# The seam between layer 0's mixing and layer 1's hop: the last tile's norm, transposes and projection reordered

## The chip, the cores and the metric

The kernel runs on one core of one Trainium2 chip. The metric is the device time of one execution in microseconds (us); it is compared by the median of several runs. The core's engines work side by side, each through its own queue in order: TensorE (PE, with its weight loads shown as PEld), VectorE (DVE), ScalarE (ACT), GpSimd (POOL) and SyncE (SP), which here only issues DMAs.

## The reference

Two layers over a graph of 2048 nodes, with 8 batches of 64 features. The adjacency is sparse (self loops, row-normalised).

```python
# layer 0: three Chebyshev terms, weights per node mixed from 16 embeddings
w = einsum('nd,dkio->nkio', embedding, weight); b = einsum('nd,do->no', embedding, bias)
As = [I, A, 2 A A - I]
x_g = einsum('knm,bmc->bnkc', As, x)
x = layernorm(x + einsum('bnki,nkio->bno', x_g, w) + b)
# layer 1: x, A x, 2 A A x - x, and again the last two, concatenated, times one weight
x = layernorm(x + concat(x, A x, 2 A A x - x, A x, 2 A A x - x) @ weight + bias)
```

So the adjacency is applied four times, one after the other: twice in layer 0 (hops 1 and 2), twice in layer 1 (hops 3 and 4). Between hops 2 and 3 stands the mixing of layer 0: for each node, 64 features of three terms times 16 weight matrices, weighted by the node's embedding and summed.

## The kernel before, in words

The function `pattern` holds the whole path that is measured. Nodes are cut into 16 tiles of 128 (NT = 16); tile t lies on the 128 partitions, with 8 x 64 features along the free dimension.

**Hops.** Hops 2 and 3 are built by `seven_products` (L586): seven products of half-size matrices in place of eight, each product in 8 steps (kk = 0 to 7). A step has parts with leads: `sum_y` (lead 5), `y_high` and `load_sum` (lead 4), `y_low` (3), `operands` (2) and `use` (0). `run` (L265) goes over the steps; at step i it issues part p of step i + lead, so a step's operands are made some steps ahead of its matmuls. `load_sum` (L636) has SP load a matrix block into a buffer of the pool `rawp` (5 buffers); `operands` (L647) casts it on ScalarE (L652) into a buffer of `spool` (4 buffers); `y_high` (L625) and `y_low` (L633) split the moving features into a high part on ScalarE (L234) and a low part on VectorE (L238); `use` (L657) issues 8 matmuls (L664). Hop 3's first product has its accumulators in `sums3[0]`; `sums3[1]` lies idle in that product, and `transpose` and `project` borrow it.

**Layer 0's mixing.** The loop at L861 goes over the tiles. `mix0` (L402) issues eight pieces of matmuls (L409) for a tile. A piece (g, i) covers batch group g. With i below 2 it is `by_batch`: its 8 weight matrices are read out of PSUM by ScalarE (L423, 8 instructions), times the embedding, into two `aside` tiles of `rawp`; GpSimd adds those up (`sum_aside`, L440, three instructions, after both such pieces of the group) and then into the sum (`add_aside`, L445). With i of 4 or 5 it is `by_four`: VectorE adds four matrices from PSUM straight into the sum (L433, 4 instructions). The list `at[n]` holds what is issued ahead of piece n: it is the order by hand of the other engines' queues. PSUM has four pairs of banks (`bank`, L84), shared by pieces, transposes, projections and hop accumulators. Tile t's operands (`operands`, L725) take a `rawp` buffer and two `spool` buffers until its last matmul.

`mix0` returns `layernorm` (L359), a generator. Its first step, right after the tile, sums (L362, L363, VectorE) and centres (L365, GpSimd). Its three further steps, called n1, n2, n3 in the loop, are issued in the next tile: n1 squares (L353, ScalarE), n2 sums them (L370, VectorE) and takes the root (L372, ScalarE), n3 takes the reciprocal (L374, VectorE) and ends on GpSimd (L375 to L380), where L380 writes the normalised tile. Then `transpose` (L303) does eight transposes on TensorE (L300), which ScalarE reads out into `hT` (L306), and `project` (L458) does 16 matmuls with layer 1's weights (L466) and six copies on ScalarE (L475).

For tiles 1 to 14 the previous tile's transposes are issued ahead of piece 7 and its projection after piece 7. The last tile, 15, is different: it issues n1, n2, n3 of tile 14 ahead of pieces 1, 2 and 3, and between them makes operands for hop 3 early (`early`, L846, moves named parts of a step forward: for steps 0 and 1 all parts but the matmuls, for steps 2, 3 and 4 the high and low parts). Tile 14's transposes are issued after step 1 of hop 3 (`last_transposed`, L791) and its projection after step 2 (`last_projected`, L794); tile 15's after steps 5 and 6. Tile 15's own n1, n2, n3 are put into `todo` (L900), from which `run` takes two entries after each step.

What sets the order: ScalarE, VectorE and GpSimd instructions marked `ordered`, and SP's loads, keep the order in which the program issues them. A pool's buffer is handed to the next tile that asks, when the work that last used it is done.

Of the kernel before, what the change touches and what calls it, by code (L numbers as in the profile page):

```python
# [20 lines left out]
NT = N // P  # L21
# [18 lines left out]
def pattern(  # L40
# [24 lines left out]
    def pool(stack, name, bufs, **kw):  # L65
        return stack.enter_context(tc.tile_pool(name=name, bufs=bufs, **kw))
# [17 lines left out]
    def bank(name):  # L84

        return psum.tile([P, 2, 512], F32, tag="ps", name=name)
# [9 lines left out]
    def bc(s, t):  # L96
        return z[s][t].rearrange("p (b c) -> p b c", c=C)
# [29 lines left out]
    def ordered(ins):  # L127
        if in_order:
            tc.keep_in_program_order(ins)
# [161 lines left out]
    def by_half(tt):  # L291
        return tt.rearrange("p j (h n) -> p h j n", h=2)

    def transposed(src, pt=None):

        pt = bank("pt") if pt is None else pt
        for j in range(B // 2):
            for h in range(2):
                q = slice(h * C, (h + 1) * C)
                nc.tensor.transpose(pt[:, h, j * C : (j + 1) * C], src[q, 2 * j * C : 2 * (j + 1) * C], ident[q, q])  # L300
        return pt[:, :, : B // 2 * C].rearrange("p h (j n) -> p h j n", n=C)

    def transpose(src, tag, pt=None):  # L303

        tt = xcpool.tile([P, B // 2, P], F32, tag="ln_xc", name=tag)
        ordered(nc.scalar.copy(by_half(tt), transposed(src, pt)))  # L306
        return tt
# [81 lines left out]
    def begin_sum(t):  # L389

        acc = work.tile([P, B, C], F32, tag="acc", name="acc")
        for g in range(2):
            ordered(nc.gpsimd.tensor_tensor(
                acc[:, 4 * g : 4 * g + 4, :].rearrange("p (j i) c -> p j i c", j=2),
                bc(0, t)[:, 4 * g : 4 * g + 4, :].rearrange("p (i j) c -> p j i c", j=2),
                ebias[:, t : t + 1, :].unsqueeze(1).to_broadcast([P, 2, 2, C]), ALU.add,
            ))
        return acc
# [59 lines left out]
    def project(t, hT, pus=None):  # L458


        for g in range(2):
            pm = bank("pu") if pus is None else pus[g]
            for i in range(2):
                for j in range(2):
                    q = slice(j * C, (j + 1) * C)
                    nc.tensor.matmul(  # L466
                        pm[:, j, i * 3 * C : (i + 1) * 3 * C], lhsT=hT[q, 2 * g + i, :], rhs=v[q],
                        start=True, stop=True,
                    )
            got = pm[:, :, : 6 * C].rearrange("p j (i k c) -> p j i k c", i=2, k=3)  # L470

            order = ["p (i j) c -> p j i c", "p (j i) c -> p j i c", "p (j i) c -> p j i c"]
            to = [bc(k, t)[:, 4 * g : 4 * g + 4, :].rearrange(order[k], j=2) for k in range(3)]
            for k in range(3):
                ordered(nc.scalar.copy(to[k], got[:, :, :, 2 - k, :]))  # L475

    def add_bias(t):
        to = bc(2, t)
        ordered(nc.vector.tensor_tensor(to, to, bias1.unsqueeze(1).to_broadcast([P, B, C]), ALU.add))
# [232 lines left out]
    def times_r(t):  # L712
        to = z2[:, t, :].rearrange("p (j n) -> p j n", n=P)
        r = rrow[:, t * P : (t + 1) * P].unsqueeze(1).to_broadcast([P, B // 2, P])
        ordered(nc.gpsimd.tensor_tensor(to, to, r, ALU.mult))  # L715
# [9 lines left out]
    def operands(t, quick=False):  # L725

        xt = work2.tile([P, B // 2, P], F32, tag="t0", name="xt")
        load(nc.sync, xt, xT[t])
        tt = [None] * 3

        def begin(k, src):
            where, tag = ((rawp, "raw"), (spool, "s"))[k != 2]
            high = hpool.tile([P, B // 2, P], F32R, tag="hl", name="hl")
            pair = where.tile([P, 2, B // 2, P], F32R, tag=tag, name="parts")
            tt[k] = [high, pair[:, 0], pair[:, 1]]
            return parts(src, tt[k], by_half if k == 1 else lambda to: to, quick)

        def of_x():
            yield from begin(0, xt)

        def of_hop(pt=None):
            yield from begin(1, transposed(z[1][t], pt))

        def of_second():
            yield from begin(2, by_pair(z[2][t]))

        return tt, of_x(), of_hop, of_second()
# [40 lines left out]
    last_h = {}  # L788
    sums3 = []

    def last_transposed(t):  # L791
        last_h["T"] = transpose(last_h[t], "hT", sums3[1][0])

    def last_projected(t):  # L794
        project(t, last_h["T"], (sums3[1][1], sums3[1][0]))
        if t < NT - 1:
            return
        layer0.close()
        t_pool = pool(tpool, "fzT", 1, reuse_waits="tile")
        for a in range(2):  # L800
            for c in range(2):
                zT[a, c] = t_pool.tile([P, 4, B * C], F32, tag=f"zT{a}{c}", name="zT")
# [22 lines left out]
    def quarter_back(a, b, which):  # L825
# [7 lines left out]
        return work_here + [lambda n=n: two(n) for n in range(0, 8, 2)]  # L833

    third = seven_products(0, to_zT, sums3, {
        (0, 1): [lambda: last_transposed(NT - 2)],
        (0, 2): [lambda: last_projected(NT - 2)],
        (0, 5): [lambda: last_transposed(NT - 1)],
        (0, 6): [lambda: last_projected(NT - 1)],
        **{(2 + t // KK, t % KK): [lambda t=t: add_bias(t)] for t in range(NT)},  # L840
        3: quarter_back(1, 1, 1), 4: quarter_back(0, 1, 0), 5: quarter_back(0, 0, 1),
    }, wait=2)
# [3 lines left out]
    def early(i, *kinds):  # L846

        got = third_got.setdefault(i, {})
        for lead, part in sorted(third[i], key=lambda part: -part[0]):
            if part.__name__ in kinds:  # L850
                part(got)
        third[i] = [part for part in third[i] if part[1].__name__ not in kinds]

    def go(it):
        return lambda: next(it)

    y, s = ("y_high", "y_low"), ("load_sum", "operands")
    acc, h, norm = first_tile[5], None, None
    tt = first_tile[0]
    coming = operands(1)  # L860
    for t in range(NT):  # L861
        got, last = {}, t == NT - 1
        at = [[] for _ in range(9)]
        n1, n2, n3 = [lambda: next(norm)] * 3 if t else [nothing] * 3

        if not last:
            following, of_x, of_hop, of_second = coming
            of_hop = of_hop()
            at[1] += [go(of_x)] * (1 if t else 3)
            at[2] += [go(of_hop), n1, go(of_hop), go(of_hop), n2]  # L870
            if t + 2 < NT:
                at[2] += [lambda: times_r(t + 2)]
                at[4] += [lambda: got.update(coming=operands(t + 2))]
            at[3] += [n3, go(of_second), lambda: got.update(acc=begin_sum(t + 1))]
            at[4] += [go(of_second), go(of_second)]
            at[6] += [(("sum", "add"), 0)]
            at[7] += [lambda: got.update(hT=transpose(h, "hT"))] if t else []
            pieces = [(0, 0), (0, 4), (0, 5), (1, 2), (0, 1), (1, 3), (1, 4), (1, 5)]
        else:
            at[1] += [n1, lambda: early(0, *y, *s)]  # L880
            at[2] += [n2, lambda: early(1, *y, *s)]
            at[3] += [n3, (("sum",), 0), lambda: early(2, *y)]
            at[4] += [lambda: early(3, *y)]
            at[5] += [lambda: early(4, *y)]
            at[6] += [(("add",), 0)]
            at[7] += [(("sum",), 1)]
            at[8] += [(("add",), 1)]
            pieces = [(0, 0), (0, 1), (0, 4), (1, 0), (0, 5), (1, 1), (1, 4), (1, 5)]
        norm_now = mix0(t, tt, acc, at, pieces)
        if 0 < t < NT - 1:  # L890
            project(t - 1, got["hT"])
        if "coming" in got:
            coming = got["coming"]
            next(coming[1])
            next(coming[1])
        norm = norm_now
        last_h[t] = h = next(norm)
        if not last:
            tt, acc = following, got["acc"]
    todo.extend([nothing] * 4 + [lambda: next(norm)] * 3)  # L900
# [425 lines left out]
def gnn_kernel(tc, x, xT, adj, diag, rcols, bias, pack, w0, out):  # L1326
    nc = tc.nc
    with tc.tile_pool(name="flag", bufs=1) as fpool:
        flag = fpool.tile([1, 1], I32, tag="flag", name="flag")
        odd = pattern(tc, x, xT, adj, diag, rcols, bias, pack, w0, out, flag)  # L1330
        with tc.If(odd > 0):
            general(tc, x, adj, bias, pack, w0, out)
# [47 lines left out]
```

## Time and profile before

| | |
|---|---|
| median of 3 runs | 765.45 us (764.99 to 766.03) |
| profiled execution, its own time | 765.98 us |
| its span, first to last instruction | 764.2 us, granted TensorE clock 0.998 |
| TensorE matmuls busy | 754.5 us (99%), 6634 instructions |
| VectorE, ScalarE, GpSimd busy | 559.0, 407.4, 269.6 us |
| tile 15 on TensorE | 509.08 to 526.1 us |
| hop 3 from its first matmul | 526.18 us |

A line of a timeline reads: start, duration, engine, line, operation, output <- inputs, partitions x elements, count; in brackets the idle time ahead and what ended it. A line of several instructions gives their common stretch. "SPq" is a DMA being issued from SP. Matmuls overlap, so the spacing of their starts, not their duration, is what one costs. The buffers' numbers are left out of names: `aside`, `raw`, `parts` and `hl` each stand for several.

### The profile page before, as it was taken

The page shows a single profiled execution, that of the slowest core. Times are in us where ns is not written, and L with a number is a line of the kernel's source. Part 1 is how long each engine was busy: PE and PEld are TensorE (multiplying, and loading weights), DVE is VectorE, ACT ScalarE, POOL GpSimd, SP SyncE. Part 2 cuts the span into 40 slices and gives each one's busy share as a digit, 9 for nine tenths or more (in the row PEclk, how much of TensorE's full clock was granted, in tenths as well). Part 3 has the DMA queues.
Part 4 walks back from the last instruction along what each step waited for, and adds up shares of the span by engine and source line. Part 5 has one row for each costly group of instructions (what it writes and reads, how often), then busy time and mean ns, then how long its engine had stood idle before and what let it go on. Part 6 is the DMA issues. An engine that isn't in the chain of part 4 may idle for free.

```text
span 764.2 us, 16926 instructions
## 1 busy us (share of the span) xinstructions
PE 754.5 (99%) x6634; PEld 658.8 (86%) x6634; DVE 559.0 (73%) x1159; ACT 407.4 (53%) x896; POOL 269.6 (35%) x297
## 2 busy tenths in 40 slices
PE   9999999999999999999999999999999999999996
PEld 6888888888889999999999999998788888888885
DVE  5768867678757888888888888875688648668663
ACT  4456533877855555555555555556887663112111
POOL 0000000000026877777788787766100000011441
PEclk9999999999999999999999999999999999999999
DMA  9998996555510000000000000002454444566631
GB/s 316 364 394 274 351 313 223 162 169 163 170 66 22 24 17 15 17 16 15 16 17 16 15 16 3 2 30 78 129 166 149 132 154 143 175 174 177 205 125 45
DMA packets 73558, 96.69 MB, mean 127 GB/s; under 512 B 4864, under 2 KB 48384, under 8 KB 73344
## 3 DMA queue, kind: packets, MB, share of 16 engines
q1 hardware_dynamic: 62064, 76.66, 31.7%
q10 hardware_dynamic: 11408, 18.89, 6.7%
q8 instruction: 54, 0.88, 0.5%
q14 instruction: 32, 0.26, 0.1%
HBM read 76.65 MB, written 18.87 MB: 125 GB/s over the span
## 4 chain that ended last, share of the span: by engine, by line
PE 95%; POOL 2%; ACT 1%; DVE 1%; DMA 0%; issue 0%; POOLq 0%; DVEq 0%
PE pm L409 34%; PE accT L664 25%; PE acc L254 15%; PE a L254 10%; PE accT L254 6%; PE pu L466 2%; PE pt L300 1%; POOL aside L440 1%; PE first L143 1%; PE accT L816 1%; ACT aside L423 1%; DMA raw<-corner 0%; POOL xc L380 0%; ACT s L652 0%; DVE acc L433 0%; ACT z L475 0%
## 5 line engine op out<-in xcount | busy, mean ns | idle before, releaser
L433 DVE SCALAR_TENSOR_TENSOR acc<-pm,pack_sb,acc 128x256 f32<-128x256 f32 x376 | 181.1, 482 | 40.1 <-PE pm L409 28.1
L664 PE MATMUL accT<-s,hl 128*128 128x512 f32 x896 | 206.6, 391 | 0.8 <-ACT s L652 0.8
L409 PE MATMUL pm<-wh,hl 64*128 64x512 f32 (+1 forms) x1332 | 204.1, 303 | 0.0
L409 PE MATMUL pm<-wm,parts 64*128 64x512 f32 (+1 forms) x1332 | 199.7, 296 | 0.0
L409 PE MATMUL pm<-wl,parts 64*128 64x512 f32 (+1 forms) x1332 | 199.6, 296 | 0.0
L664 PEld LDWEIGHTS accT<-s,hl 128*128 128x128 f32 x896 | 167.3, 188 | 36.7 <-ACT s L652 1.2
L652 ACT CAST s<-raw 128x1024 fp32r<-128x1024 bf16 x104 | 110.0, 1058 | 43.4 <-ACT hl L234 23.4
L409 PEld LDWEIGHTS pm<-wh,hl 64*128 64x128 f32 x1332 | 126.8, 187 | 4.6 <-issue 0.4
L409 PEld LDWEIGHTS pm<-wl,parts 64*128 64x128 f32 x1332 | 126.7, 187 | 4.3
L409 PEld LDWEIGHTS pm<-wm,parts 64*128 64x128 f32 x1332 | 126.4, 187 | 4.4
L254 PE MATMUL acc<-hl,s 128*128 128x512 f32 x512 | 116.9, 390 | 0.0
L254 PEld LDWEIGHTS acc<-hl,s 128*128 128x128 f32 x512 | 96.3, 188 | 20.5 <-ACT hl L234 0.3
L423 ACT ACTIVATE aside<-pm,pack_sb 128x128 f32<-128x128 f32 x272 | 74.2, 389 | 48.1 <-PE pm L409 48.0
L715 POOL TENSOR_TENSOR z<-z,rrow 128x512 f32<-128x512 f32 x16 | 21.0, 1314 | 212.5 <-DVE z L688 212.5
L234 ACT CAST hl<-z 128x256 fp32r<-128x256 f32 (+1 forms) x96 | 48.0, 519 | 60.7 <-PE acc L254 24.9
L440 POOL TENSOR_TENSOR aside<-aside 128x1024 f32<-128x1024 f32 (+2 forms) x51 | 75.1, 1473 | 2.7
L254 PE MATMUL a<-hl,s 128*128 128x512 f32 (+1 forms) x352 | 73.4, 370 | 0.0
L254 PEld LDWEIGHTS a<-hl,s 128*128 128x128 f32 x352 | 61.9, 188 | 11.3
L320 POOL TENSOR_TENSOR parts<-parts 128x512 fp32r<-128x512 f32 x45 | 58.3, 1297 | 34.9 <-DVE parts L314 27.3
L238 DVE TENSOR_TENSOR hl<-z,hl 128x512 fp32r<-128x512 f32 (+1 forms) x96 | 53.8, 567 | 18.6 <-ACT hl L234 15.8
L287 POOL TENSOR_TENSOR z<-z,got 128x512 f32<-128x512 f32 x3 | 4.8, 1617 | 142.6 <-ACT got L286 142.6
L254 PE MATMUL accT<-hl,s 128*128 128x512 f32 x192 | 44.3, 390 | 0.0
(136 smaller groups left out, 814.2 us busy)
## 6 DMA issues: line engine op xcount, KB each, us to landing
raw<-in_adj SPq DMA_DIRECT2D x58, 512.0 KB, 5.9
raw<-sums_of SPq DMA_DIRECT2D x64, 256.0 KB, 2.8
sums_of<-z ACTq DMA_DIRECT2D x16, 512.0 KB, 6.6
raw<-quarters SPq DMA_DIRECT2D x32, 256.0 KB, 2.7
raw<-in_adj SPq DMA_DIRECT2D x16, 384.0 KB, 3.4
quarters<-seen ACTq DMA_DIRECT2D x16, 256.0 KB, 6.0
xt<-in_xT SPq DMA_DIRECT2D x16, 256.0 KB, 2.6
z<-in_x SPq DMA_DIRECT2D x15, 256.0 KB, 7.0
```

Of the source, the lines that this page charges most:

```text
L234: ordered(nc.scalar.copy(to[0], src))
L238: ordered(nc.vector.tensor_tensor(to[1], src, to[0], ALU.subtract))
L254: nc.tensor.matmul(accs[i], lhsT=s[:, i * P : (i + 1) * P], rhs=hl[h], start=(first and h == 0), stop=(last and h == 1),)
L320: ordered(nc.gpsimd.tensor_tensor(mixed, mixed, low, ALU.add))
L409: nc.tensor.matmul(pm[:, j], lhsT=tt[k][n][q, lhsT, :], rhs=w_parts[n][k][q, ds, :], start=(k == 0 and n == 0), stop=(k == 2 and n == 2),)
L423: ordered(nc.scalar.activation(aside[g][d // DG][:, d % DG, :, i, :], pm[:, :, d, :], AF.Copy, scale=e(d)))
L433: ordered(nc.vector.scalar_tensor_tensor(part, got, e(dg * DG + d), part, ALU.mult, ALU.add))
L440: ordered(nc.gpsimd.tensor_tensor(to, to, more, ALU.add))
L466: nc.tensor.matmul(pm[:, j, i * 3 * C : (i + 1) * 3 * C], lhsT=hT[q, 2 * g + i, :], rhs=v[q], start=True, stop=True,)
L652: ordered(nc.scalar.copy(s, got["raw"]))
L664: nc.tensor.matmul(acc[i][:, c], lhsT=hl[h][:, i * P : (i + 1) * P], rhs=S[:, c * 512 : (c + 1) * 512], start=(kk == 0 and h == 0), stop=( ...
L715: ordered(nc.gpsimd.tensor_tensor(to, to, r, ALU.mult))
```

## The change

Tile 14's n1 and n2 are both issued ahead of the last tile's piece 1, and n3 ahead of piece 2. Its transposes move from hop 3's step 1 into the tile, ahead of piece 6, and its projection from step 2 to the end of the tile, with PSUM pairs of their own (`pt`, `pu`) in place of the borrowed ones. The early operands of hop 3 are spread: step 0's high part, load and cast ahead of piece 2, its low part ahead of piece 3, step 1's ahead of pieces 4 and 5, highs and lows of steps 2 and 3 ahead of pieces 6 to 8. Step 4's are no longer made early. Tile 15's transposes and projection stay where they were.

```diff
-    def last_transposed(t):
-        last_h["T"] = transpose(last_h[t], "hT", sums3[1][0])
+    def last_transposed():
+        last_h["T"] = transpose(h, "hT", sums3[1][0])
...
     third = seven_products(0, to_zT, sums3, {
-        (0, 1): [lambda: last_transposed(NT - 2)],
-        (0, 2): [lambda: last_projected(NT - 2)],
-        (0, 5): [lambda: last_transposed(NT - 1)],
-        (0, 6): [lambda: last_projected(NT - 1)],
+        (0, 5): [last_transposed],
+        (0, 6): [last_projected],
...
         else:
-            at[1] += [n1, lambda: early(0, *y, *s)]
-            at[2] += [n2, lambda: early(1, *y, *s)]
-            at[3] += [n3, (("sum",), 0), lambda: early(2, *y)]
-            at[4] += [lambda: early(3, *y)]
-            at[5] += [lambda: early(4, *y)]
-            at[6] += [(("add",), 0)]
-            at[7] += [(("sum",), 1)]
-            at[8] += [(("add",), 1)]
+            at[1] += [n1, n2]
+            at[2] += [n3, lambda: early(0, "y_high", *s)]
+            at[3] += [(("sum",), 0), lambda: early(0, "y_low")]
+            at[4] += [lambda: early(1, "y_high", *s)]
+            at[5] += [lambda: early(1, "y_low")]
+            at[6] += [(("add",), 0), lambda: got.update(hT=transpose(h, "hT")), lambda: early(2, "y_high")]
+            at[7] += [(("sum",), 1), lambda: early(2, "y_low"), lambda: early(3, "y_high")]
+            at[8] += [(("add",), 1), lambda: early(3, "y_low")]
             pieces = [(0, 0), (0, 1), (0, 4), (1, 0), (0, 5), (1, 1), (1, 4), (1, 5)]
         norm_now = mix0(t, tt, acc, at, pieces)
-        if 0 < t < NT - 1:
+        if t:
             project(t - 1, got["hT"])
```

More of the change, by code (lines that the diff above doesn't have):

```diff
@@ L789, in pattern, with last_projected @@
     sums3 = []
-    def last_transposed(t):
-        last_h["T"] = transpose(last_h[t], "hT", sums3[1][0])
[L794 to L797, printed above, removed]
+    def last_transposed():
+        last_h["T"] = transpose(h, "hT", sums3[1][0])
+    def last_projected():
+        project(NT - 1, last_h["T"], (sums3[1][1], sums3[1][0]))
         layer0.close()
@@ L855, in go @@
         return lambda: next(it)
-    y, s = ("y_high", "y_low"), ("load_sum", "operands")
+    s = ("load_sum", "operands")
     acc, h, norm = first_tile[5], None, None
@@ L896, in pattern @@
         norm = norm_now
-        last_h[t] = h = next(norm)
+        h = next(norm)
         if not last:
```

## The prediction

> **What bounds the kernel now.** I read the page first (busy shares, chain that ended last), then TensorE's waits and timeline where the change lies (505 to 556 us), then the other engines' timelines there.
>
> ```profile
> PE 754.5 (99%) x6634; PEld 658.8 (86%) x6634; DVE 559.0 (73%) x1159; ACT 407.4 (53%) x896; POOL 269.6 (35%) x297
> ...
> PE 95%; POOL 2%; ACT 1%; DVE 1%; DMA 0%; issue 0%; POOLq 0%; DVEq 0%
> ```
>
> TensorE is busy 99% of the span and is 95% of the chain. From 545 us to its last matmuls at 757 us the view of waits lists none for it: whatever moves TensorE's start of step 7 of the third hop's first product (545.38 us) moves the end by as much. So the question is when that step starts. TensorE's timeline, columns start and duration:
>
> ```profile
> 530.03 0.46 PE L300 MATMUL accT<-ident,xc 64*128 64x64 f32 x8
> 530.42 2.11 PE L664 MATMUL accT<-s,hl 128*128 128x512 f32 x8
> 532.76 1.57 PE L466 MATMUL accT<-v,hT 64*128 64x192 f32 x16 [0.24 <-ACT hT L306]
> 534.26 3.92 PE L664 MATMUL accT<-s,hl 128*128 128x512 f32 x16
> 538.99 2.11 PE L664 MATMUL accT<-s,hl 128*128 128x512 f32 x8 [0.81 <-ACT s L652]
> 541.44 0.46 PE L300 MATMUL accT<-ident,xc 64*128 64x64 f32 x8 [0.34 <-POOL xc L380]
> 541.83 2.12 PE L664 MATMUL accT<-s,hl 128*128 128x512 f32 x8
> 543.88 1.57 PE L466 MATMUL accT<-v,hT 64*128 64x192 f32 x16
> 545.38 10.95 PE L664 MATMUL accT<-s,hl 128*128 128x512 f32 x47
> ```
>
> The reader is to see tile 14's transposes (530.03) and projection (532.76), tile 15's (541.44 and 543.88), and three waits. By starts, a matmul of L664 costs (10.95 - 0.39) / 46 = 0.23; in a row 0.227, so a step of eight is 1.82, and 1.93 where it follows a 64-row group (its first is 0.11 longer). In a tile the same two groups are cheaper:
>
> ```profile
> 486.51 0.41 PE L300 MATMUL pt<-ident,xc 64*128 64x64 f32 x8
> 486.72 0.36 PE L409 MATMUL pm<-wh,hl 64*128 64x256 f32 x2
> ...
> 488.95 1.47 PE L466 MATMUL pu<-v,hT 64*128 64x192 f32 x16
> 490.12 0.53 PE L409 MATMUL pm<-wh,hl 64*128 64x512 f32 x2
> ```
>
> Start to start, transposes 0.21 (0.39 in the hop), projection 1.17 (1.50). Last, GpSimd, VectorE, SP and ScalarE in tile 15:
>
> ```profile
> 522.95 4.65 POOL L440 TENSOR_TENSOR aside<-aside 128x1024 f32<-128x1024 f32 x3
> ```
>
> ```profile
> 523.95 1.69 DVE L238 TENSOR_TENSOR hl<-z,hl 128x256 fp32r<-128x256 f32 x1
> 525.56 4.18 DVE L433 SCALAR_TENSOR_TENSOR acc<-pm,pack_sb,acc 128x256 f32<-128x256 f32 x8
> ```
>
> ```profile
> 525.38 0.32 SPq L123 DMA_DIRECT2D raw<-corner  x1
> ```
>
> ```profile
> 528.10 1.05 ACT L652 CAST s<-raw 128x1024 fp32r<-128x1024 bf16 x1 [3.94 <-DMA raw<-corner]
> ```
>
> The first add of sum_aside(0) ends at 525.36. Two things were waiting for that: VectorE's low half (1.69 where its like take 0.42) and SP's load, which takes that add's buffer and lets ScalarE cast 2.72 later. The raw pool's five buffers go out in program order: step 0's load stood on SP, idle since 455 us, until 510.72, when tile 14's last add (510.70) had freed the buffer whose turn it was.
>
> **What the Trainium skill says.** "SBUF — State Buffer", section "SBUF: two separate sides": VectorE and GpSimd share a port pair as an exclusive lock, which a VectorE operation with two SBUF inputs needs against a GpSimd operation that reads SBUF, and the loser waits the whole instruction. The trace agrees (1.69); L433, which reads PSUM, ran at 0.48 beside the same adds. "TensorE: Matmul & The Clock Gate", section "Part 3: Packing small matmuls — row/col tiling": matmuls on different row groups overlap; the trace's 64-row pairs start 0.003 to 0.007 apart. "DMA: Bandwidth & Descriptors", section "Latency and other measured facts": some 2 us fixed per DMA; here corner loads land after 2.6 to 2.7 us alone, up to 4.8 in a burst.
>
> **The change part by part**, on the clock of the profiled run.
>
> Up to piece (1,1) TensorE is as before: pieces take 2.05 to 2.17 and (1,1) ends at 521.78. The transposes go in there (521.99), (1,4) and (1,5) end at 526.31, and the projection would end at 527.48. Tile 14's work thus costs 0.21 + 1.17 instead of 0.39 + 1.50, and saves 0.5, with the stalls before L466 (0.4) and L664 (0.95) and the extra starts. The upper bound: 527.48 + 0.08, six steps 1.93 + 5 x 1.82, transposes 0.48, step 6 with its gap 2.05, projection 1.50 gives 542.6, a gain of 2.8.
>
> Norm first. Squares at 513.51 as before, VectorE's sum 514.22 to 514.90, the root 514.94: ScalarE idles 0.75, but two casts no longer stand ahead, so (0,1) starts at 515.15 (before 515.28). Reciprocal at 515.3; GpSimd's end of the norm takes 2.46 from there (499.78 to 502.24), so tile 14 is ready at 517.8, where before 522.98. The transposes at 521.8 never wait. sum_aside(0) follows at once, 5.1 earlier; its first add, 2.4, ends at 520.2.
>
> Operands spread. ScalarE: (0,1) to 517.2, high 0 and cast 0 (0.29 + 0.95) to 518.4, (1,0) eight by 0.25 to 520.4, high 1 to 520.7. Now step 1's load is moved past the two `aside` tiles of piece (1,0). Program order, oldest freed first: these take tile 14's operand buffer and step 0's, and the load gets the buffer of sum_aside(0)'s first add. It is issued at 520.2 and the cast starts at 520.2 + 2.72 = 522.9: **ScalarE waits 2.2 us** for it. Queued behind are (1,1) (523.9 to 526.0), the transposes' eviction hT (done 526.46), highs 2 and 3. TensorE's projection starts at 526.5, 0.2 late.
>
> Then GpSimd starts sum_aside(1) at 526.1, first add to 528.5. High 2 is there at 526.8, so VectorE's low 2 loses the port and runs after 528.5; behind it stand the four L433 of (1,5), 528.7 to 530.8. Four PSUM pairs exist; the projection takes two, so the hop's first accumulators get those of (1,4) and (1,5). TensorE starts step 0 at 526.5 + 1.17 + 0.08 = 527.75, does its first four matmuls to 528.75, and **waits 2.05 us** for (1,5), to 530.8.
>
> After that nothing is late. Four matmuls to 531.8, five steps to 540.9, transposes 541.4, step 6 543.45, projection 544.95. The projection's six copies stand on ScalarE from 527.4 to 529.1 (1.76), with casts 2 and 3 behind them, needed only at 533.6. Tile 15's norm: add 531.55, sums and centring to 533.7, squares to 534.4, then 4.7 as before (536.67 to 541.38): 539.1, in time for 540.9. Loads of steps 2 to 4 take buffers freed by 528.5 and land by 531.5; their casts come at 529.5 to 533. ScalarE sheds hT and six copies (0.5 + 1.6) from the hop; step 5's cast ends near 536.8 for a start at 539.1. early(4) left out is one 0.3 cast and a low half one step later, hidden by the hop's 1.82 against 1.25 of ScalarE per step; without that cover, 0.3.
>
> Sum: 545.38 - 544.95 = **0.4 us gained**. The profiled run took 765.98 at a span of 764.2 (1.8 around it); it stands 0.5 above the median 765.45. 765.98 - 0.4 = 765.6 there, and **765.0** against the median.
>
> Unknown is what the trace can't name: which buffer and which PSUM pair each tile gets. Bounds: +0 to 2.8 gained, and below nothing only through the length of the hold.
>
> **Rivals.** (a) The add's buffer goes to `aside` and step 1's load gets another, because the add's end counts before step 0's cast. Then (1,0)'s second half waits for 520.4, (1,1) ends at 524.85, the first add of sum_aside(1) at 527.35, (1,5) at 529.65; TensorE waits 1.1, and step 7 starts at 543.83: 1.55 gained, 763.9. For it: both ends lie within 2 us; against: the cast comes first in program and time. (b) Step 0's second half gets a pair that a projection copy frees earlier, not (1,5)'s: no 2.05 wait; step 7 at 542.8, or 543.2 if tile 15's norm (539.1) is then late: 2.2 gained, up to 2.8 without the hold; 763.0. For it: first projection copies end 0.5 before (1,5)'s evictions in tile 14 (509.70 against 510.16). (c) Slower: the load of step 1 lands late, as in a burst, 4.8 instead of 2.65. All of (1,1), hT, sum_aside(1), low 2 and (1,5) shift one to one: -0.4 + 2.15 = 1.7 lost, 767.2. It turns to a loss from a landing of 3.05 us. Against it: SP has that load alone. (d) The program's order on TensorE comes out otherwise and nothing moves: 765.45.
>
> **How the numbers follow.** A measurement of this kernel can tell about 0.2%, 1.5 us, from no change. Forecast 42%, (a) 20%, (b) 24%, (c) 8%, (d) 6%. Faster by over that: all of (b), half of (a) at its edge, 6 of the forecast's 42 for durations 1 us better: 40%. Slower: (c) and 2 of the forecast's: 10%. Same: the rest, 50%. The forecast alone spans 764.3 to 765.8; the range goes to 762.9 for (b), and to 766.3, leaving out most of (c).
>
> **What would show it.** Right: tile 14's L380 near 516.8; the transposes before (1,4) and L466 at 526.5 under the name pu; a ScalarE wait of about 2 us for `raw` ahead of the second cast; an L238 of some 2 us; a TensorE wait on VectorE in the middle of step 0; no wait on s L652 before step 5. Wrong: no ScalarE wait for `raw` before (1,1) means (a), no TensorE wait in step 0 means (b), step 7 after 546 us means (c).

## The result, and the profile after

The changed kernel takes 764.31 us (median; 763.44 to 765.01), the kernel before 765.47 on the same chip. The ratio is 0.9985, with a 95% interval of 0.9979 to 0.9992: about 1.15 us faster, between 0.6 and 1.6. The profiled execution took 764.04 at a span of 762.3, with a granted TensorE clock of 0.999. The forecast was 765.0; rival (a) gave 763.9.

The page of the changed kernel shows the same bound. TensorE's share of the chain rises from 95% to 98%, and GpSimd has left the chain:

```profile
PE 753.6 (99%) x6634; PEld 660.6 (87%) x6634; DVE 560.2 (73%) x1159; ACT 406.7 (53%) x896; POOL 269.7 (35%) x297
...
PE 98%; DVE 1%; issue 0%; ACT 0%; DVEq 0%
```

TensorE's timeline of the changed kernel, from tile 14's transposes on (start, duration, line, tiles, count, and in brackets the idle time ahead):

```profile
521.67 0.41 PE L300 MATMUL pt<-ident,xc 64*128 64x64 f32 x8
...
526.28 1.47 PE L466 MATMUL pu<-v,hT 64*128 64x192 f32 x16
527.69 1.20 PE L664 MATMUL accT<-s,hl 128*128 128x512 f32 x4
529.65 10.24 PE L664 MATMUL accT<-s,hl 128*128 128x512 f32 x44 [0.76 <-DVE acc L433]
539.81 0.46 PE L300 MATMUL accT<-ident,xc 64*128 64x64 f32 x8
540.21 2.11 PE L664 MATMUL accT<-s,hl 128*128 128x512 f32 x8
542.25 1.57 PE L466 MATMUL accT<-v,hT 64*128 64x192 f32 x16
```

Three waits of the kernel before are gone (0.24 before the projection, 0.81 before step 5, 0.34 before tile 15's transposes). One new wait stands in the middle of hop 3's step 0, after its first four matmuls: 0.76 in brackets. By starts it is longer: four matmuls (0.11 + 4 x 0.227 = 1.02) from 527.69 reach 528.71, and the next starts at 529.65, so it costs 0.94. The lines of the other three engines say where it comes from. ScalarE:

```profile
517.34 1.10 ACT L652 CAST s<-raw 128x1024 fp32r<-128x1024 bf16 x1
518.29 1.20 ACT L423 ACTIVATE aside<-pm,pack_sb 128x128 f32<-128x128 f32 x4
520.27 1.14 ACT L423 ACTIVATE aside<-pm,pack_sb 128x128 f32<-128x128 f32 x4 [0.79 <-POOL aside L440]
...
521.67 1.05 ACT L652 CAST s<-raw 128x1024 fp32r<-128x1024 bf16 x1
522.62 2.17 ACT L423 ACTIVATE aside<-pm,pack_sb 128x128 f32<-128x128 f32 x8
524.63 0.64 ACT L306 COPY hT<-pt 128x512 f32<-128x512 f32 x1
```

GpSimd:

```profile
517.60 4.82 POOL L440 TENSOR_TENSOR aside<-aside 128x1024 f32<-128x1024 f32 x3
522.50 0.80 POOL L445 TENSOR_TENSOR acc<-acc,aside 128x256 f32<-128x256 f32 x1
524.87 4.63 POOL L440 TENSOR_TENSOR aside<-aside 128x1024 f32<-128x1024 f32 x3 [1.57 <-ACT aside L423]
```

VectorE:

```profile
526.30 1.24 DVE L238 TENSOR_TENSOR hl<-z,hl 128x256 fp32r<-128x256 f32 x1
527.47 2.03 DVE L433 SCALAR_TENSOR_TENSOR acc<-pm,pack_sb,acc 128x256 f32<-128x256 f32 x4
```

Read together: ScalarE's second half of piece (1,0) waits for GpSimd's first add (0.79 at 520.27), not the second cast for its load (521.67, no wait). That is rival (a)'s sign. sum_aside(1) starts at 524.87. The low half of step 2 wants VectorE 1.4 later, while GpSimd's first add is running, and takes 1.24 where its like take 0.42. The four L433 of piece (1,5) stand behind it, and TensorE's step 0 waits for the PSUM pair that they read.

Between two profiles the start of tile 15, where nothing is changed yet, differs by up to 0.76 us (508.32 to 509.08), and the stretch behind the last matmul by up to 0.53 (6.93 to 7.46). So stages are compared below from that start to step 7 of the third hop's first product, called the **seam**. From step 7 to the start of the last matmul it is 211.55 to 211.60 in all ten kernels of this study, so between the tile's start and the last matmul the seam is the whole difference. It is 36.30 before and 34.78 after: 1.52 gained in these two traces, inside the 0.6 to 1.6 of the medians.

### The profile page after: what moved, and what is told of

Its sections match the earlier page's. It is cut to its first block, busy times and chain, and to the rows that moved or that the text cites. A ratio compares the mean times of both kernels' runs of the same rounds, so it can differ in the third digit from the quotient of the medians.

```text
span 762.3 us, 16926 instructions
## 1 busy us (share of the span) xinstructions
PE 753.6 (99%) x6634; PEld 660.6 (87%) x6634; DVE 560.2 (73%) x1159; ACT 406.7 (53%) x896; POOL 269.7 (35%) x297
## 4 chain that ended last, share of the span: by engine, by line
PE 98%; DVE 1%; issue 0%; ACT 0%; DVEq 0%
PE pm L409 36%; PE accT L664 27%; PE acc L254 15%; PE a L254 10%; PE accT L254 6%; PE pu L466 2%; PE pt L300 1%; PE first L143 1%; PE accT L814 1%; DVE acc L433 1%; PE accT L466 0%; PE accT L153 0%; PE accT L300 0%; ACT sq L994 0%; DVE z L289 0%
## 5 line engine op out<-in xcount | busy, mean ns | idle before, releaser
L433 DVE SCALAR_TENSOR_TENSOR acc<-pm,pack_sb,acc 128x256 f32<-128x256 f32 x376 | 181.0, 482 | 44.0 <-PE pm L409 32.0
L409 PE MATMUL pm<-wh,hl 64*128 64x512 f32 (+1 forms) x1332 | 208.0, 303 | 0.0
L409 PE MATMUL pm<-wm,parts 64*128 64x512 f32 (+1 forms) x1332 | 203.5, 296 | 0.0
L409 PE MATMUL pm<-wl,parts 64*128 64x512 f32 (+1 forms) x1332 | 203.4, 296 | 0.0
L409 PEld LDWEIGHTS pm<-wh,hl 64*128 64x128 f32 x1332 | 130.9, 187 | 4.0 <-issue 0.4
L409 PEld LDWEIGHTS pm<-wl,parts 64*128 64x128 f32 x1332 | 130.8, 187 | 3.7
L409 PEld LDWEIGHTS pm<-wm,parts 64*128 64x128 f32 x1332 | 130.5, 187 | 3.8
L254 PEld LDWEIGHTS a<-hl,s 128*128 128x128 f32 x352 | 61.9, 188 | 11.3
```

The costliest lines, as they stand in the source:

```text
L254: nc.tensor.matmul(accs[i], lhsT=s[:, i * P : (i + 1) * P], rhs=hl[h], start=(first and h == 0), stop=(last and h == 1),)
L409: nc.tensor.matmul(pm[:, j], lhsT=tt[k][n][q, lhsT, :], rhs=w_parts[n][k][q, ds, :], start=(k == 0 and n == 0), stop=(k == 2 and n == 2),)
L433: ordered(nc.vector.scalar_tensor_tensor(part, got, e(dg * DG + d), part, ALU.mult, ALU.add))
```

## The experiments

My theory after the two traces: the gain is what is left of the forecast's upper bound once the hold of VectorE's low half by the port pair that VectorE and GpSimd share is taken off, and that hold is the whole rest. The rivals: ScalarE's wait for a buffer costs by itself; or the place of the transposes and the projection, or the norm alone, makes the gain. Each ratio compares with the kernel before on the same chip (its median was 765.59 beside the first four experiments, 765.39 beside the last four). Since these differ, the experiments are compared with each other by their seams, each from one trace.

| kernel | median, us | ratio (95%) | seam, us |
|---|---|---|---|
| before | 765.47 | 1 | 36.30 |
| changed | 764.31 | 0.9985 (0.9979 to 0.9992) | 34.78 |
| low2_behind | 762.93 | 0.9966 (0.9954 to 0.9978) | 33.81 |
| late_casts | 763.03 | 0.9969 (0.9958 to 0.9980) | 34.07 |
| late_and_low2 | 763.34 | 0.9971 (0.9959 to 0.9983) | 33.83 |
| bunched | 764.84 | 0.9994 (0.9986 to 1.0002) | 35.73 |
| norm_only | 766.24 | 1.0012 (1.0005 to 1.0019) | 37.12 |
| back_in_hop | 764.47 | 0.9987 (0.9981 to 0.9994) | 35.34 |
| move_only | 765.22 | 0.9998 (0.9990 to 1.0007) | 36.23 |
| hold_on_load | 765.77 | 1.0005 (0.9999 to 1.0012) | 36.63 |

**low2_behind: the low half of step 2 behind the evictions of (1,5).**

```diff
-            at[7] += [(("sum",), 1), lambda: early(2, "y_low"), lambda: early(3, "y_high")]
-            at[8] += [(("add",), 1), lambda: early(3, "y_low")]
+            at[7] += [(("sum",), 1), lambda: early(3, "y_high")]
+            at[8] += [lambda: early(2, "y_low"), (("add",), 1), lambda: early(3, "y_low")]
```

> Step 2's low half is issued behind piece (1,5)'s four evictions instead of ahead of them; nothing else changes. Theory: in the changed kernel that low half loses the shared port to the first add of sum_aside(1), 0.8 us, keeps (1,5) in PSUM until 529.5, and TensorE waits 0.94 us in the middle of step 0. Behind the evictions it blocks nobody: no TensorE wait in step 0, step 7 at 542.8 instead of 543.75, 0.9 us below the changed kernel, 763.4. Rival, that (1,5)'s evictions are late because ScalarE's wait for an aside buffer delays the whole tile: they start no earlier, the wait stays, 764.3.

Measured: 762.93, 0.5 below the 763.4 expected, and without the wait in step 0, as the theory had it; seam 33.81. VectorE goes from (1,4) straight to (1,5), eight L433 in a row, and the low halves come after:

```profile
523.89 4.20 DVE L433 SCALAR_TENSOR_TENSOR acc<-pm,pack_sb,acc 128x256 f32<-128x256 f32 x8 [1.63 <-PE pm L409]
528.01 2.15 DVE L238 TENSOR_TENSOR hl<-z,hl 128x256 fp32r<-128x256 f32 x2
```

TensorE has no wait left; the six steps run as one group of 48:

```profile
525.84 1.47 PE L466 MATMUL pu<-v,hT 64*128 64x192 f32 x16
527.24 11.22 PE L664 MATMUL accT<-s,hl 128*128 128x512 f32 x48
538.39 0.46 PE L300 MATMUL accT<-ident,xc 64*128 64x64 f32 x8
```

And ScalarE still waits, in this kernel even twice:

```profile
519.82 1.14 ACT L423 ACTIVATE aside<-pm,pack_sb 128x128 f32<-128x128 f32 x4 [0.79 <-POOL aside L440]
520.84 0.42 ACT L234 CAST hl<-z 128x256 fp32r<-128x256 f32 x1
522.04 1.05 ACT L652 CAST s<-raw 128x1024 fp32r<-128x1024 bf16 x1 [0.78 <-DMA raw<-corner]
```

What follows: 0.97 of the seam hung on the place of one VectorE instruction; the wait in step 0 was priced at 0.94. Two waits of ScalarE, 1.6 together, cost TensorE nothing here. So in the changed kernel ScalarE's wait mattered only in that it moved GpSimd's add over the low half. (The second wait is for step 1's load, which took 4.00 to land here and 3.18 in the changed kernel's trace.)

**late_casts: the two loads moved behind the `aside` tiles of (1,0), their casts behind (1,1).**

```diff
-            at[2] += [n3, lambda: early(0, "y_high", *s)]
+            at[2] += [n3, lambda: early(0, "y_high")]
...
-            at[4] += [lambda: early(1, "y_high", *s)]
+            at[4] += [lambda: early(1, "y_high"), lambda: early(0, "load_sum"), lambda: early(1, "load_sum")]
...
-            at[6] += [(("add",), 0), lambda: got.update(hT=transpose(h, "hT")), lambda: early(2, "y_high")]
+            at[6] += [(("add",), 0), lambda: got.update(hT=transpose(h, "hT")), lambda: early(2, "y_high"), lambda: early(0, "operands"), lambda: early(1, "operands")]
```

> The loads of steps 0 and 1 are issued ahead of piece (0,5) and their casts ahead of (1,4), so that the aside tiles of (1,0) are handed out before them and should not wait for GpSimd. Step 2's low half stays ahead of (1,5). Theory: ScalarE's 0.8 us wait in the middle of (1,0) is gone, (1,1) ends near 524.0 and sum_aside(1) starts 0.7 earlier, its first add ends near 526.6; the low half still waits for it, but TensorE's wait in step 0 falls from 0.94 to about 0.3: 0.6 us below the changed kernel, 763.7. Rival, that the buffer wait costs nothing because the port decides: wait and time as in the changed kernel, 764.3.

Measured: 763.03 (763.7 expected), seam 34.07. No `aside` tile waits any more; (1,1) starts at 521.43, 12.92 after the tile's start where the changed kernel has 13.65. (That is what the 0.79 wait alone would give, 12.86; that the casts were moved as well brought no more.) Step 2's low half stays ahead of (1,5), but meets GpSimd at the end of an add and not at its start:

```profile
525.85 0.53 DVE L238 TENSOR_TENSOR hl<-z,hl 128x256 fp32r<-128x256 f32 x1
526.31 2.03 DVE L433 SCALAR_TENSOR_TENSOR acc<-pm,pack_sb,acc 128x256 f32<-128x256 f32 x4
```

What follows: the hold falls from 0.8 to 0.1, and 0.71 of the seam with it; by starts some 0.2 to 0.3 of TensorE's wait in step 0 is left, as expected. The same wait can be cleared wholly by the order of VectorE, or for the most part by the hand-out of buffers.

**late_and_low2: both edits.**

```diff
...
-            at[4] += [lambda: early(1, "y_high", *s)]
+            at[4] += [lambda: early(1, "y_high"), lambda: early(0, "load_sum"), lambda: early(1, "load_sum")]
...
-            at[8] += [(("add",), 1), lambda: early(3, "y_low")]
+            at[8] += [lambda: early(2, "y_low"), (("add",), 1), lambda: early(3, "y_low")]
```

> Both edits together: late loads and casts of steps 0 and 1, and step 2's low half behind (1,5). Theory: both act on the same TensorE wait, which either nearly removes, so together they give 0.9 us, not 1.5: 763.4, no TensorE wait from the tile to step 5. Rival, that they are separate costs: 762.8.

Measured: 763.34, as expected; seam 33.83, as low2_behind. The two edits don't add: they act on one and the same wait. So 33.8 is what this order of TensorE takes with no wait in it.

**bunched: norm ahead and transposes and projection in the tile, but the operands where they were before.**

```diff
-            at[1] += [n1, n2]
-            at[2] += [n3, lambda: early(0, "y_high", *s)]
-            at[3] += [(("sum",), 0), lambda: early(0, "y_low")]
+            at[1] += [n1, n2, lambda: early(0, *y, *s)]
+            at[2] += [n3, lambda: early(1, *y, *s)]
+            at[3] += [(("sum",), 0), lambda: early(2, *y)]
...
```

> The changed kernel with the operands of hop 3 where they were before: all of step 0 ahead of piece 1, all of step 1 ahead of piece 2, highs and lows of steps 2, 3 and 4 ahead of pieces 3, 4 and 5. Norm, transposes and projection as in the changed kernel. Theory: spreading is the part that loses; bunched, no low half stands ahead of (1,5) while sum_aside(1) runs, so (1,5) leaves PSUM at 528.5 and TensorE does not wait: step 7 near 542.9, 763.4. Rival, that spreading is what lets ScalarE keep up: pieces (0,1) and (1,0) are read out later, (1,1) ends after 525, sum_aside(1) and tile 15's norm follow late, and the time is at or above the changed kernel's 764.3.

Measured: 764.84, seam 35.73: about 1.4 us worse than I had expected. VectorE of this kernel:

```profile
518.15 2.45 DVE L238 TENSOR_TENSOR hl<-z,hl 128x256 fp32r<-128x256 f32 x1 [2.77 <-ACT hl L234]
520.52 2.03 DVE L433 SCALAR_TENSOR_TENSOR acc<-pm,pack_sb,acc 128x256 f32<-128x256 f32 x4
```

and TensorE:

```profile
522.70 0.46 PE L300 MATMUL pt<-ident,xc 64*128 64x64 f32 x8 [1.49 <-DVE acc L433]
```

With the norm ahead GpSimd's sum_aside(0) runs from 517.91. The low half of step 1, which stood harmlessly on VectorE before, now comes 0.24 later and is held until the first add ends (520.32). Behind it stand the evictions of (0,4), and TensorE's next PSUM pair. The time is the rival's, at or above the changed kernel's, but not for the rival's reason: it looked for the price of bunching on ScalarE, and it lay on VectorE, ahead of (0,4).

**norm_only: only the norm ahead.**

```diff
-            at[1] += [n1, lambda: early(0, *y, *s)]
-            at[2] += [n2, lambda: early(1, *y, *s)]
-            at[3] += [n3, (("sum",), 0), lambda: early(2, *y)]
+            at[1] += [n1, n2, lambda: early(0, *y, *s)]
+            at[2] += [n3, lambda: early(1, *y, *s)]
+            at[3] += [(("sum",), 0), lambda: early(2, *y)]
```

The diff is against the kernel before.

> The kernel before with one part of the change: tile 14's n1, n2 ahead of piece 1 and n3 ahead of piece 2. Transposes and projection stay in the hop, operands stay bunched. Theory: the early norm lets sum_aside(0) start 5 us sooner, so loads, casts and tile 15's norm come sooner and the three TensorE waits of the hop (0.4, 0.95, 0.5 us) go; but the bunched low half of step 1 then meets sum_aside(0) ahead of (0,4)'s evictions, as in the bunched run, and costs TensorE 0.8 to 1.5 us in the tile. Left: 0.5 to 1.0 us below before, 764.6. Rival, that the gain is the move of tile 14's transposes and projection: 765.5, as before.

Measured: 766.24, ratio 1.0012: slower than before, and I had expected a gain. The block is the one of bunched; TensorE shows

```profile
522.66 0.39 PE L409 MATMUL pm<-wh,hl 64*128 64x256 f32 x2 [1.48 <-DVE acc L433]
...
541.50 0.46 PE L300 MATMUL accT<-ident,xc 64*128 64x64 f32 x8 [0.32 <-POOL xc L380]
```

The early norm does remove the wait ahead of the hop's projection (0.31 by starts) and cuts step 5's from 1.06 to 0.4. But the hold lengthens the tile on TensorE from 17.10 to 18.85, and tile 15's transposes wait as before. The seam is 0.82 longer. I had priced the block at 0.8 to 1.5 and taken all three waits of the hop for gone; the block was dearer, and one of them stayed whole, one in part.

**back_in_hop: norm ahead and operands spread, transposes and projection back in the hop.**

```diff
-            at[6] += [(("add",), 0), lambda: got.update(hT=transpose(h, "hT")), lambda: early(2, "y_high")]
+            at[6] += [(("add",), 0), lambda: early(2, "y_high")]
...
-        (0, 5): [last_transposed],
+        (0, 1): [lambda: last_transposed(NT - 2)],
+        (0, 2): [lambda: last_projected(NT - 2)],
+        (0, 5): [lambda: last_transposed(NT - 1)],
...
```

The diff is against the changed kernel.

> The changed kernel with tile 14's transposes and projection back in the hop (after steps 1 and 2, in the borrowed pairs); norm ahead and operands spread as changed. Theory: moving them saves 0.5 us but hands step 0 the PSUM pair of (1,5) and so costs the 0.94 us wait; undone, step 0 does not wait, and the time is 0.4 below the changed kernel, 763.9. Rival, that the move is what gains: 765 or more.

Measured: 764.47, seam 35.34. Neither number came true: I had expected a gain of 0.4 on the changed kernel, the rival a loss of 0.7 or more. By the seams of the two traces it loses 0.56; the medians, 764.47 and 764.31, don't tell the two apart (ratios to the kernel before 0.9987 and 0.9985, with overlapping intervals). As the theory had it, TensorE has neither the wait in step 0 nor one ahead of the projection. What it had overlooked is that tile 15's transposes wait again. (The low half of step 2 is held here too, and (1,5) is evicted only by 529.5; that step 0, from 525.50, doesn't wait for it fits that no tile `pu` takes a pair here, so that step 0 gets other pairs.) TensorE's timeline:

```profile
531.78 1.57 PE L466 MATMUL accT<-v,hT 64*128 64x192 f32 x16
533.28 6.20 PE L664 MATMUL accT<-s,hl 128*128 128x512 f32 x24
539.82 0.46 PE L300 MATMUL accT<-ident,xc 64*128 64x64 f32 x8 [0.34 <-POOL xc L380]
```

ScalarE shows why:

```profile
532.75 1.75 ACT L475 COPY z<-accT 128x256 f32<-128x256 f32 x6 [1.05 <-PE accT L466]
534.34 0.69 ACT L353 ACTIVATE sq<-xc 128x512 f32<-128x512 f32 x1
...
536.28 1.04 ACT L652 CAST s<-raw 128x1024 fp32r<-128x1024 bf16 x1
```

In the hop the projection's six copies stand ahead of tile 15's squares (534.34, that is 25.94 after the tile's start, where the changed kernel's come at 532.62, 23.65 after it), and of step 5's cast. Of these 2.3, some 1.7 are the copies: the centred tile lay ready at 532.65. The other 0.6 come from step 1's load, which landed late here (3.79 us). That cast ends at 537.32, and by starts step 5 is 0.39 late; the transposes are 0.41 late. Without these 0.80 the seam with the work in the hop would be 34.5, against 33.8 in the tile: the place itself is worth 0.7.

**move_only: only transposes and projection into the tile.**

```diff
-            at[6] += [(("add",), 0)]
+            at[6] += [(("add",), 0), lambda: got.update(hT=transpose(h, "hT"))]
...
-        if 0 < t < NT - 1:
+        if t:
             project(t - 1, got["hT"])
```

The diff is against the kernel before; the hop's two entries for tile 14 are gone too.

> The kernel before with the other part alone: transposes and projection of tile 14 in the last tile; n1, n2, n3 stay ahead of pieces 1, 2, 3 and the operands bunched. Theory: the norm is ready at 523.0, so the transposes stop TensorE 1.3 us in the tile; sum_aside stays late, tile 15's norm is ready at 541.4 as before and its transposes wait for it, so nothing is gained: 765.4. Rival, that the move is what gains: 764.3 or less.

Measured: 765.22, seam 36.23, as expected. The transposes now come before their norm is ready, and two of the hop's waits stay:

```profile
PE pt L300 <- POOL xc L380: 1.1, 1, 1.1
PE accT L664 <- ACT s L652: 0.4, 1, 0.4
PE accT L300 <- POOL xc L380: 0.3, 1, 0.3
```

(TensorE's waits in the seam: total, times, longest.)

**hold_on_load: the forecast's assignment made to happen.** Step 0's high half, load and cast go one piece earlier, so that the `aside` tiles of (1,0) take step 0's buffer and step 1's load is left with the add's.

```diff
-            at[1] += [n1, n2]
-            at[2] += [n3, lambda: early(0, "y_high", *s)]
+            at[1] += [n1, n2, lambda: early(0, "y_high", *s)]
+            at[2] += [n3]
```

> The changed kernel with step 0's high half, load and cast issued ahead of piece (0,1) instead of ahead of (0,4). Its buffer is then free before sum_aside(0)'s first add ends, goes to the second aside tile of (1,0), and step 1's load gets the add's buffer: the assignment that the forecast took. Theory: ScalarE then waits for that load, 2 us or more, ahead of (1,1); (1,1), sum_aside(1), the low half of step 2 and (1,5) follow one to one, TensorE waits some 2.5 us in step 0, and step 7 stands 36.3 us behind the tile's start as in the kernel before: 765.4. Rival, that such a hold is covered: 764.3 as the changed kernel.

Measured: 765.77, ratio 1.0005, seam 36.63: the gain is gone. ScalarE waits for the load, which SP issues at 520.33:

```profile
522.93 1.05 ACT L652 CAST s<-raw 128x1024 fp32r<-128x1024 bf16 x1 [2.75 <-DMA raw<-corner]
523.89 2.17 ACT L423 ACTIVATE aside<-pm,pack_sb 128x128 f32<-128x128 f32 x8
```

and TensorE twice, in the places that the forecast named:

```profile
526.58 1.57 PE L466 MATMUL pu<-v,hT 64*128 64x192 f32 x16 [0.78 <-ACT hT L306]
528.09 1.20 PE L664 MATMUL accT<-s,hl 128*128 128x512 f32 x4
530.87 10.22 PE L664 MATMUL accT<-s,hl 128*128 128x512 f32 x44 [1.59 <-DVE acc L433]
```

These are nearly the forecast's own clock times, by coincidence: this trace's tile starts 0.76 earlier than that of the kernel before, and sum_aside(0) starts 9.58 after it instead of the forecast's 8.72, since step 0's cast now delays piece (0,1) on ScalarE. Without that 0.86 the seam would be about 35.8 (an estimate from these two numbers); the forecast had 544.95 - 509.08 = 35.87.

## Why the prediction was right, and where it was wrong

The time fell into the forecast's band of "same" (less than 0.2% from before) and into its range, but not by the forecast's mechanism: what happened is rival (a), which I had given 20%. The forecast's own number, 765.0, gave 0.4 of the 1.15 us gained. That band and range held is owed to the rivals priced into them, and in part to luck: rival (a) lay on the band's edge.

**The step that failed** is the sentence "Program order, oldest freed first: these take tile 14's operand buffer and step 0's, and the load gets the buffer of sum_aside(0)'s first add." In the changed kernel the second `aside` tile of (1,0) waits for the add, and step 1's load is issued at 518.47, as soon as step 0's cast has ended (518.44). So ScalarE waits 0.79 and not 2.2: the load is no longer behind the add, and its landing is covered. It is covered only just: it landed at 521.65, and the cast started at 521.67. hold_on_load shows that the rest of the forecast's chain was sound: where the load does get the add's buffer, the wait is 2.75, it runs through hT, sum_aside(1), the low half and (1,5) to TensorE, and nothing is gained; with the 0.86 of its other delay taken off, the estimate is 0.5 gained (36.30 - 35.8), near the forecast's 0.4. Why the pool handed out the add's buffer in one kernel and the cast's in the other, with the cast ahead of the add in program order and in time in both (by 1.8 us in the changed kernel, by 4.6 in hold_on_load), no run tells; that stays open.

The forecast also put little on a late landing (rival (c)), since SP has step 1's load alone. That reason doesn't hold: issued alone, this load took 3.18 to land in the changed kernel, 4.00 in low2_behind and 3.79 in back_in_hop, where the forecast took 2.65. In all three a 16 KB packet of the instruction queue starts while the load is on its way; that this is the cause was not tested.

Rival (a), as worked out, against the trace after, counted from the tile's start:

| | rival (a) | trace |
|---|---|---|
| second half of (1,0) starts | 11.3 | 11.30 |
| (1,1) ends | 15.8 | 15.82 |
| first add of sum_aside(1) ends | 18.3 | 18.29 |
| (1,5) evicted | 20.6 | 20.53 |
| TensorE's wait in step 0 | 1.1 | 0.94 |
| step 7 | 34.75 | 34.78 |

Its 1.55 us gained were 1.52 in the trace; in medians 1.15, with 0.6 to 1.6 as bounds.

**Right, by steps.** Step 7 carries the end one to one (211.6 in ten kernels). The norm ends 8.7 after the tile's start, as forecast (517.8 - 509.08; the trace's L380 ends at 517.64, and 517.64 - 508.97 = 8.67). Transposes and projection cost 0.21 and 1.17 in the forecast's tile; here the projection, followed by the hop, takes 1.41 to the next start, 0.16 above the 1.17 + 0.08 used. The upper bound of 2.8 was 2.5 in the trace of low2_behind (36.30 - 33.81). The lacking 0.3 is that 0.16 and another 0.12 in the six steps (11.15 from start to start where 11.03 were worked out). Two slips in the forecast's sums move nothing: without the hold its own terms give 542.9, not 542.8, and the stall before the hop's projection is 0.31 by starts, not 0.4.

**The pair of PSUM banks.** Rival (b), in which step 0 never waits for (1,5), didn't happen: the second half of step 0 does wait for (1,5)'s evictions. low2_behind reaches (b)'s size (763.0 forecast, 762.93 measured) in another way, by making those evictions earlier.

**The port.** The Trainium skill, "SBUF — State Buffer", section "SBUF: two separate sides", has the loser of the shared port pair blocked for the other's whole instruction. The traces agree: 2.45 for a low half of 0.42 that came 0.24 after the start of a 2.4 add (bunched), 1.24 for one that came 1.4 after (changed). L433, with PSUM among its inputs, took 2.03 to 2.04 for four beside the same adds, as it did with no add running (2.04 at 515.59), so it isn't held. Moving a low half behind it cost nothing here. The traces show the lock from the other side too: in the changed kernel sum_aside(0)'s first add starts at 517.60, while a low half runs (517.55 to 517.97), and takes 2.64; in hold_on_load, with no low half beside it, it takes 2.41. That 0.2 is part of ScalarE's wait of 0.79, and the forecast had left it out.

**What the whole gain is made of**, from the seams. Before, TensorE's waits by starts are 0.31 (projection), 0.96 and 0.10 (step 5) and 0.41 (tile 15's transposes): 1.78. Without them the seam would be 34.5, which back_in_hop without its waits gives as well. In the tile, without waits, it is 33.8 (low2_behind). So 1.78 of waits are removed and 0.7 is gained by the place, against 0.94 of a new wait: 1.5 gained. No part does it alone: the norm ahead alone loses 0.82, the move alone gains 0.07, both without the spreading gain 0.57, the norm and the spreading without the move gain 0.96. (The spreading alone, and with the move alone, was not run.) The early norm makes the adds start 5 us sooner, and only the spreading takes low halves out of their way; one of them was left in it.

## What to carry to other kernels

When GpSimd work is moved, go through VectorE's queue for instructions with two SBUF inputs that now come during it, and see what stands behind each: an eviction of PSUM there turns a 2 us hold into a wait of TensorE. Put such an instruction behind the evictions that are due (here one line, 762.93, 0.34% below the kernel before with 0.22 to 0.46 as bounds, and better than both kernels). Where two tiles ask a pool for buffers in turn, work out both hand-outs and price each. Here the dearer one was the one with a DMA behind the release (a seam of about 35.8 by the estimate above, against 34.78), and in late_casts the loads were moved so that neither occurred (34.07).

## What the runs showed that I had not expected

A VectorE instruction held by GpSimd's first add doesn't wait for the next ones: in the changed kernel the add ends at 527.26 and the low half at 527.54, while the second add, recorded from 527.34, ends at 528.69 and the third at 529.50. So a hold lasts to the end of one instruction, not of the row of three.

The forecast took the first matmul after a 64-row group to cost 0.11 more. At the seam between tile and hop it is dearer: the projection followed by step 0 took 1.40 to 1.42 in low2_behind, the changed kernel and bunched, where the same 16 matmuls followed by a 64-row piece took 1.17.
